# Finishing the last projections, and loading the gates, at other steps of a fused attention and FFN kernel

## The chip, the cores and the metric

The kernel runs on one core of one Trainium2 chip. The metric is the time of one execution on the device in microseconds (us), the median of several runs. TensorE (PE) multiplies matrices into PSUM; VectorE (DVE) and ScalarE (ACT) read PSUM and SBUF; GpSimd (POOL) works on SBUF; SyncE (SP) issues all DMA transfers of this kernel, one after the other, each after the waits that it carries.

## The reference

The input x has 1024 tokens of 512 channels. With xn = layernorm(x), the result is

```python
s = attention(xn)          # 32 query heads, 8 key/value heads, head size 128
g = silu(ffn(xn))          # dequantized gate, up and down matrices, 1792 wide
out = x + s * g
```

Attention normalizes queries and keys by RMS with weights, adds a linear bias in the distance of the positions (ALiBi) under a causal mask, and projects the heads' outputs by Wo. All is float32 in the reference. The kernel writes every float32 operand of a matmul as a sum of two 16-bit numbers, high and low, and multiplies three of the four products (`mm3`, lines 112 to 116).

## The kernel before

The work stands in three stages. The FFN comes first (until 217 us in the profile); its silu is written to the DRAM scratch `gd`. Then come twelve projections of 8 tiles each (128 tokens, 12 matmuls of 128x512): for each of four pairs of key heads one `kv` and two `q` projections, kv0, q0, q1, kv1 and so on to q7. Then comes attention in 256 steps; a step is one query tile of one head. The first eight steps are interleaved with the last two projections (q6 and q7), two tiles to a step.

**Weights of the next projection.** `prepare(k + 1, t)` (L672) is called ahead of tile t of projection k. It holds a small table by t: at t = 1 `norms` (ones times the squared weights, on PE, into a PSUM bank that `spare` (L486) gives, and `am`, the scale, on DVE), from t = 2 on `split_head`, one head a tile: ACT writes the high half `wh` (L561), DVE the low half `wl` (L562). `squares` for the projection after that runs on ACT at t = 6. The tiles of a projection use two PSUM tags of two banks each, "m" for even and "o" for odd tiles; `spare` takes a bank of "m" too.

**Finishing of a projection's tiles.** ACT copies a tile from PSUM to `f` (L580, three buffers of four tiles). `queue_half` (L767) then puts off, by counts of steps, `inverse` and `newton` (the reciprocal root of the norm), `normalize` (POOL, L636) and `halves` (DVE: the cast to the high half at L648, the subtraction to the low half at L649, into an `a16` buffer of five). For all but the last projection the pair is then transposed by DMA (L657) and stored to `qd` or `kd` (L662, L664). The last projection (q7, the queries of the last group of heads) is not stored: its pairs stay in SBUF until `last_queries` (L817) transposes them at the steps of `LAST_QUERIES`. When they are made is written out by hand in `LAST_ROOTS` and `LAST_PAIRS`, step numbers by half and by tile.

**Attention.** There are eight groups of heads of 32 steps each: group g has steps 32g to 32g + 31. A group takes four blocks of 256 queries (`qb`), in the order 2, 3, 0, 1 (group 7: 2, 3, 1, 0). Step n does: scores on PE (L114 to L116) into the PSUM tag "s"; one step later the minimum with the bias on DVE (L878, 256 instructions in all, by which a step can be found in the profile) and the exponential on ACT (L879); then the high half on ACT (L898) and the low half on DVE (L907) in a `p16` buffer of five; then a DMA transpose of the pair to `pT` (L915, or L910 for block 0, where POOL first clears a part of the buffer at L894); nine steps after the scores PE multiplies by the values (`av`). The output projection `op` follows, and DVE adds it to y.

**Gates.** For each block `gate_load(qb)` (L959) loads 0.5 MB of `gd` and 0.5 MB of x by two DMAs (L962, L963) at the step in `GATE_LOADS`, and `gate_partial` multiplies y by the gate and adds x, four POOL instructions (L969, L970) from the step in `GATE_SUMS`. Both lists follow the last group's order of blocks, 2, 3, 1, 0. A load uses one of the three `f` buffers. The order on each engine and in SP's queue is the program's own order; no scheduler changes it.

## Time and profile before

| what | value |
|---|---|
| time, three runs | 1067.37, 1065.36, 1066.66 us (median 1066.66) |
| profiled execution, own time | 1066.42 us |
| its span, first to last instruction | 1064.6 us |
| PE busy | 1002.7 us (94%) |
| DVE busy | 886.1 us (83%) |
| ACT busy | 802.7 us (75%) |
| POOL busy | 413.9 us (39%) |
| hardware DMA queue (SP) | 203.21 MB, 85.4% of 16 engines |

The page's first part gives the busy time of each engine, summed over all stages. PE is idle for 62 us of the span, and the question is where. The view by windows puts 17.3 us of that into the first 200 us (FFN), which the change does not touch; the rest lies in the projections, where attention fills up, and in the last 60 us.

The time outside the span is 1066.42 - 1064.6 = 1.8 us; it is taken as the same before and after.

### The profile page before, as it was taken

To read this page: it belongs to the slowest core of one execution; us is meant where nothing else is said; L and a number is where in the kernel's file an instruction comes from. 1 tells how busy PE (TensorE), PEld (TensorE's weight loads), DVE (VectorE), ACT (ScalarE), POOL (GpSimd) and SP (SyncE) were. 2 spreads that over 40 slices of the span, in tenths; PEclk is the share of its full clock that TensorE was granted. 3 is DMA by queue.
4 is the path that set the end of the run, shared out by engine and by line. 5 is a ranking of instruction groups with operands and counts; after the bars stand their busy time and mean duration, and the time that the engine had idled before them with its cause. 6 is when DMAs were issued, how large, how long until landed. Compare 5 with 4: busy or idle time off the path is not lost.

```text
span 1064.6 us, 18405 instructions
## 1 busy us (share of the span) xinstructions
PE 1002.7 (94%) x5913; PEld 584.6 (55%) x5913; DVE 886.1 (83%) x1745; ACT 802.7 (75%) x2160; POOL 413.9 (39%) x407
## 2 busy tenths in 40 slices
PE   7899899999989999898799999999999999999986
PEld 4344377844444444344566666566666666665563
DVE  7888996638778687788799899898998998979986
ACT  5777644778877787587778788797987888868862
POOL 2588653124545546361343215123141141250732
PEclk9999999999999999999999999999999999999998
DMA  6123259447988989989999999899999998999995
GB/s 202 49 100 119 70 170 302 166 139 162 219 228 188 242 203 235 279 179 207 226 193 214 195 200 222 167 227 197 189 207 193 197 223 182 221 224 194 231 189 129
DMA packets 455039, 204.39 MB, mean 192 GB/s; under 512 B 401506, under 2 KB 411038, under 8 KB 454942
## 3 DMA queue, kind: packets, MB, share of 16 engines
q1 hardware_dynamic: 454942, 203.21, 85.4%
q8 instruction: 46, 0.75, 0.3%
q14 instruction: 51, 0.42, 0.1%
HBM read 77.32 MB, written 27.27 MB: 98 GB/s over the span
## 4 chain that ended last, share of the span: by engine, by line
PE 48%; DVE 17%; ACT 13%; issue 10%; DMA 8%; SPq 2%; POOL 2%; DVEq 0%; ACTq 0%; POOLq 0%
PE gu_ps L267 6%; DMA pT<-p 4%; PE s L114 4%; DVE pf L878 3%; PE s L116 3%; PE s L115 3%; PE op L114 3%; PE op L115 3%; PE av L114 3%; PE op L116 3%; PE av L116 3%; PE av L115 3%; ACT p L898 2%; ACT pf L879 2%; PE ps_q L114 2%
## 5 line engine op out<-in xcount | busy, mean ns | idle before, releaser
L907 DVE SCALAR_TENSOR_TENSOR p<-pf,row,p 128x1024 f16<-128x1024 f32 (+7 forms) x256 | 227.8, 890 | 23.5 <-ACT p L898 20.3
L879 ACT ACTIVATE pf<-pf,row 128x1024 f32<-128x1024 f32 (+7 forms) x256 | 197.6, 772 | 57.2 <-DVE row L878 52.7
L878 DVE CUSTOM_DVE_ANT_0 pf<-s,trel,cs 128x1024 f32<-128x1024 f32 (+7 forms) x256 | 207.2, 809 | 13.7 <-PE s L116 13.4
L898 ACT ACTIVATE p<-pf,row 128x1024 f16<-128x1024 f32 (+7 forms) x256 | 196.5, 768 | 8.4 <-DMA pT<-p 3.5
L114 PE MATMUL av<-pT,vT 128*128 128x256 f16 (+1 forms) x640 | 167.8, 262 | 15.5 <-DMA pT<-p 15.5
L115 PE MATMUL av<-pT,vT 128*128 128x256 f16 (+1 forms) x640 | 167.8, 262 | 0.0
L116 PE MATMUL av<-pT,vT 128*128 128x256 f16 (+1 forms) x640 | 167.6, 262 | 0.0
L114 PE MATMUL s<-kT,qT 128*128 128x512 f16 (+3 forms) x384 | 125.0, 325 | 12.4 <-DVE row L878 12.1
L115 PE MATMUL s<-kT,qT 128*128 128x512 f16 (+3 forms) x384 | 125.0, 326 | 0.0
L116 PE MATMUL s<-kT,qT 128*128 128x512 f16 (+3 forms) x384 | 123.4, 326 | 0.0
L837 POOL TENSOR_SCALAR wor<-wor,rvs 128x512 f32<-128x512 f32 x32 | 54.5, 1702 | 162.8 <-DMA wor<-in_wo 141.5
L114 PE MATMUL ps_q<-wh_q,xth 128*128 128x512 f16 x256 | 97.6, 381 | 2.6 <-DVE am_q L526 2.5
L116 PE MATMUL ps_q<-wh_q,xtl 128*128 128x512 f16 x256 | 97.5, 381 | 0.0
L115 PE MATMUL ps_q<-wl_q,xth 128*128 128x512 f16 x256 | 97.5, 381 | 0.0
L114 PE MATMUL op<-woh,oh 128*128 128x512 f16 x248 | 94.5, 381 | 0.0
L115 PE MATMUL op<-wol,oh 128*128 128x512 f16 x248 | 94.3, 380 | 0.0
L116 PE MATMUL op<-woh,ol 128*128 128x512 f16 x248 | 94.2, 380 | 0.0
L114 PEld LDWEIGHTS <-vT 128*128 128x128 f16 x640 | 62.6, 98 | 56.6 <-DMA pT<-p 9.4
L115 PEld LDWEIGHTS <-vT 128*128 128x128 f16 x640 | 62.6, 98 | 41.3 <-issue 3.5
L941 ACT ACTIVATE oh<-av 128x256 f16<-128x256 f32 x128 | 47.7, 373 | 48.5 <-PE av L116 47.8
L636 POOL TENSOR_TENSOR f_q<-f_q,inv_q 128x512 f32<-128x512 f32 x64 | 77.4, 1237 | 1.1
L844 POOL TENSOR_TENSOR wol<-wor,woh 128x512 f16<-128x512 f32 x32 | 49.4, 1543 | 71.3 <-ACT woh L843 71.3
(194 smaller groups left out, 2255.6 us busy)
## 6 DMA issues: line engine op xcount, KB each, us to landing
qd<-tr_q SPq DMA_DIRECT2D x56, 256.0 KB, 3.4
qT<-qd SPq DMA_DIRECT2D x28, 512.0 KB, 4.5
wq<-in_wq SPq DMA_DIRECT2D x32, 256.0 KB, 3.9
wo_sq<-in_wo SPq DMA_DIRECT2D x8, 1024.0 KB, 9.1
wor<-in_wo SPq DMA_DIRECT2D x32, 256.0 KB, 3.7
gui<-in_gu_w SPq DMA_DIRECT2D x13, 512.0 KB, 3.5
wkv<-in_wkv SPq DMA_DIRECT2D x16, 256.0 KB, 3.8
vd<-v SPq DMA_DIRECT2D x8, 512.0 KB, 4.0
```

What stands on the lines that cost most here:

```text
L114: te.matmul(ps, lhsT=lh, rhs=rh, start=first, stop=False)
L115: te.matmul(ps, lhsT=lh, rhs=rl, start=False, stop=False)
L116: te.matmul(ps, lhsT=ll, rhs=rh, start=False, stop=last)
L267: te.matmul(banks[j][:, k, :], lhsT=w[:, j, ws], rhs=x[:, j, k * 512 : k * 512 + 512], start=x is xth, stop=x is xtl)
L636: ge.tensor_tensor(f, f, ib, ALU.mult)
L837: ge.tensor_scalar(wor[g, i], wor[g, i], rvs[:, g : g + 1], None, ALU.mult)
L844: ge.tensor_tensor(wol[g, i], raw, woh[g, i], ALU.subtract)
L878: ve.tensor_tensor_reduce(p, ps, trel[g][:, S - w :], cs[:, hh : hh + 1], 3e38, ALU.add, ALU.min, least[:, c])
L879: se.activation(p, p, AF.Exp, bias=least[:, c], scale=-1.0, accum_out=total[:, c])
L898: se.activation(p16[u, qt][:, :, 0, :], pf[u, qt], AF.Copy, scale=scale[:, qt : qt + 1])
L907: ve.scalar_tensor_tensor(lo, p, scale, hi, ALU.mult, ALU.subtract)
L941: se.activation(oh, av_ps[u], AF.Copy, scale=1.0 / P_SCALE)
```

## The change

It has five edits.

- `prepare`: every entry of the table but `squares` comes one tile later (`norms` at t = 2, `scale` at 3, `factors` at 7, `split_head` from 3, `split_values` from 5). The calls for projection 0, inside the FFN, are shifted by one so that they stay where they were.
- `spare`: the bank for `norms` is one of the scores' tag "s" for projections 1 to 10, and one of "o" for projection 11.
- `queue_half`: half 1 of q6 (the last but one projection, tiles 4 to 7) is finished at steps 28 (roots) and 36, 44, 52 and 60 (pairs), no more during q7. That moves its four DMA transposes and four stores as well.
- `LAST_ROOTS`, `LAST_PAIRS`: the roots of q7 move from steps 24 and 36 to 66 and 70, its pairs from 46, 78, 110, 142, 174, 221, 224, 229 to 76, 88, 100, 112, 124, 136, 148, 160. All eight are then held at once, so `halves` takes three of the buffers from the tag "tr", which nothing else uses by then.
- `GATE_LOADS`, `GATE_SUMS`, `gate_load`: loads for blocks 2, 3, 1, 0 at steps 194, 203, 211, 219 instead of 211, 219, 235, 251; sums at 221, 229, 244, 237 instead of 227, 235, 251, 259. Block 0's load has a buffer of its own.

```diff
-LAST_ROOTS = {1: 24, 0: 36}
-LAST_PAIRS = {4: 46, 5: 78, 6: 110, 7: 142, 2: 174, 3: 221, 0: 224, 1: 229}
+LAST_ROOTS = {1: 66, 0: 70}
+LAST_PAIRS = {4: 76, 5: 88, 6: 100, 7: 112, 2: 124, 3: 136, 0: 148, 1: 160}
+
+LATE_ROOTS = 28
+LATE_PAIRS = [36, 44, 52, 60]
...
-GATE_LOADS = [211, 219, 235, 251]
-GATE_SUMS = [227, 235, 251, 259]
+GATE_LOADS = [194, 203, 211, 219]
+GATE_SUMS = [221, 229, 244, 237]
...
     def spare(k, name):
-        return ps1("m", name) if k else pair(name)[:, 0, :]
+        if k == 0:
+            return pair(name)[:, 0, :]
+        return ps2(name)[:, 0, :] if k < len(projections) - 1 else ps1("o", name)
...
-                a16 = fq.tile([P, 2, n, HD], F16, tag="a16", name=f"q16_{self.i}_{t}", bufs=5)
+                tag = "tr" if self.k == len(projections) - 1 and t in (0, 1, 3) else "a16"
+                a16 = fq.tile([P, 2, n, HD], F16, tag=tag, name=f"q16_{self.i}_{t}", bufs=5)
...
-            elif t == 1:
+            elif t == 2:
                 p.norms()
-            elif t == 2:
+            elif t == 3:
                 p.scale()
-            elif t == 6:
+            elif t == 7:
                 p.factors()
-            if 2 <= t < 2 + p.n:
-                p.split_head(t - 2)
-            elif p.kind == "kv" and 4 <= t < 6:
-                p.split_values(t - 4)
+            if 3 <= t < 3 + p.n:
+                p.split_head(t - 3)
+            elif p.kind == "kv" and 5 <= t < 7:
+                p.split_values(t - 5)
...
         last = p is projections[-1]
+        late = p is projections[-2] and half == 1
 
         def due(steps, i, f):
-            if last and i is None:
+            if late:
+                c = TILES + (LATE_ROOTS if i is None else LATE_PAIRS[i] - 4)
+            elif last and i is None:
                 c = TILES + LAST_ROOTS[half]
...
-        gx = fq.tile([P, 2, NQT, DM], F32, tag="f", name=f"gx{qb}", bufs=3)
+        pool, tag, bufs = (fq, "f", 3) if qb else (late[0], "gx", 1)
+        gx = pool.tile([P, 2, NQT, DM], F32, tag=tag, name=f"gx{qb}", bufs=bufs)
```

More of the change, by code (lines that the diff above doesn't have):

```diff
@@ L707, in attention_gated_by_ffn_kernel @@
         if it == NI - 4:
-            prepare(0, 1)
+            prepare(0, 2)
         if it == NI - 3:
@@ L750, in attention_gated_by_ffn_kernel @@
                 elif NI - 6 <= it < NI - 1:
-                    prepare(0, 8 - NI + it)
+                    prepare(0, 9 - NI + it)
                 if it == NI - 2:
```

## The prediction

> **What bounds the kernel now.** Read first the page's busy times: PE works 1002.7 of 1064.6 us, so it is the bound nearly everywhere, and only PE's own idle time can be won. Next come PE's waits. Among the longest are:

> ```profile
> PE av L114 <- DMA pT<-p: 15.5, 14, 2.7
> PE s L114 <- DVE row L878: 12.1, 19, 1.8
> PE n_ps L518 <- DVE v L595: 5.6, 3, 2.7
> ...
> PE ps_q L114 <- DVE am_q L526: 2.5, 2, 1.2
> ```

> The last two are in the projections, the first two where attention fills up and at its end. The timeline of PE places them:

> ```profile
> 305.03 0.17 PE L518 MATMUL n_ps<-sb_q,ones_bf 128*128 128x4 bf16 x1 [1.46 <-DVE v L595]
> ...
> 309.05 0.38 PE L114 MATMUL ps_q<-wh_q,xth 128*128 128x512 f16 x1 [1.24 <-DVE am_q L526]
> ...
> 440.07 0.16 PE L518 MATMUL n_ps<-sb_q,ones_bf 128*128 128x4 bf16 x1 [2.71 <-DVE v L595]
> ...
> 440.50 0.63 PE L115 MATMUL ps_q<-wl_q,xth 128*128 128x512 f16 x1
> ```

> `norms` of the next projection stands between tiles 0 and 1 and wants a bank of "m" that tile 6 of the kv projection before still holds; then tile 2 waits for the bank of `norms`. The pair of waits comes again at 371.71 and 375.72.

> The steady groups of attention are read by windows, one a block of eight steps. Group 3 (steps 96 to 111):

> ```profile
> 685.54:702.04 16.50, 16.50 (x118) 10.47 (x117) 16.21 (x35) 15.07 (x33) 2.72 (x1) 1.00 1.05 207
> 702.04:725.08 23.04, 23.04 (x159) 14.58 (x157) 22.38 (x37) 19.76 (x35) 10.33 (x6) 1.00 1.07 218
> ```

> The columns are the window's length, then PE, weight loads, DVE, ACT and POOL busy, clock, DMA share, GB/s. PE is full, and DVE lacks only 0.29 and 0.66 us of it. In the other two blocks of the group DVE has 3.67 and 1.42 us left.

> **1. Projections.** PE's waits for banks after kv1, kv2 and kv3 are 1.46 + 1.24, the same again, and 2.71 us; with two of 0.26 us at other starts they are 8.6 us. After the last one the clock is 0.50 from 439.40 to 442.82, and the matmul takes 0.63 instead of 0.38 us. PE is busy 2.75 us there, so half of it, 1.4 us, is lost: 10.0 us in all. [...] This trace shows it halved after gaps of 2.71 us and of 2.66 us (below). [...] The wait itself goes: "s" is idle in projections 1 to 9, and for projection 11 the bank of "o" that is asked for at t = 2 was freed by tile 7 a tile earlier.

> What is late next is `wl`. Against the start of PE's next projection the last L562 ends 0.7 us early after each kv (300.08 for 300.82), and 2.75 to 4.2 us early elsewhere, 1.6 at q7. One tile is 2.59 us. The fourth head comes a tile later, but most of what stands ahead of it in DVE's queue was not waiting for PE: at t = 5 DVE has one L562 less to do before it, and the added step ahead of it is 0.42 + 0.41 + 0.69 us (L595, L648, L649) beside ACT's evacuation of a tile, about 1.1 us (L580, L582, L594). I put 0.7 us of new wait on each of q2, q4, q6 and q7's start, 3 us; ends 0 and 7. **Net -7 us**, ends -10 and -3.

> **2. Where attention fills up.** DVE and ACT, between steps 4 and 5:

> ```profile
> 478.82 1.25 DVE L648 CAST q<-f_q 128x512 f16<-128x512 f32 x1 [2.72 <-POOL f_q L636]
> 480.10 1.41 DVE L649 TENSOR_TENSOR q<-f_q,q 128x512 f16<-128x512 f32 x1
> 481.43 1.26 DVE L648 CAST q<-f_q 128x512 f16<-128x512 f32 x1
> ...
> 484.40 1.28 DVE L878 CUSTOM_DVE_ANT_0 pf<-s,trel,cs 128x1024 f32<-128x1024 f32 x1
> ...
> 485.72 1.15 ACT L879 ACTIVATE pf<-pf,row 128x1024 f32<-128x1024 f32 x1 [4.35 <-DVE row L878]
> ```

> DVE finishes q6's tiles 4, 5, 6 (5.6 us, after 2.7 us of waiting for POOL), and ACT idles 4.35 us for the minimum behind them. All of that leaves. PE pays for it later: its waits for L878 from 485.74 to 503.90 are 0.36, 0.80, 1.42, 1.82 and 0.28, together 4.7 us. The transposes' waits after that (505.49 to 522.68: 0.45, 2.57, 2.32, 0.38) stay: ACT stands 1.41 and 2.52 us before L843 for POOL's scaling of Wo, which waits for its load. q6's four transposes and four stores also leave SP's queue there. **-4 us**, ends -8 (part of the transposes' waits too) and 0 (ACT or the loads hold it all).

> **3. The pairs' new places.** A pair costs DVE 0.42 + 0.69 us in quiet, 1.26 + 1.41 while POOL works. Group 1 gets four and loses one. Two of them fall at steps 36 and 44, where DVE is nearly full, two into blocks with 3.8 and 1.4 us left; four transposes and four stores come too, each with an SP issue of about 1.3 and 0.6 us and landing 3 to 4 us later; nobody waits for them before group 6. **+0.8 us**, ends 0 and +3. Groups 2 to 5 get eight for four (+4.4 us of DVE); only 76, 100, 136 and 160 fall into full blocks, where 78, 110, 142 and 174 stood. **+0.5**, ends -2 and +3. Three leave groups 6 and 7: the block with step 221 takes 16.26 us and the one with 224 and 229 takes 17.37, where groups without them take 13.5 and 16.5. The gates' sums stay there, so of 3.6 us I count **-1.3**, ends -3 and 0.

> **4. Gates.** Two loads of 1 MB move from steps 235 and 251 into steps 194 and 203, ahead of transposes in SP's queue where the DMA share is 1.05 already. Next row: the load at 994.31 delayed the transpose behind it to 7.6 us from a usual 3 to 4. A transpose there has five steps (10 us or more) until PE needs it, so most is covered: **+1**, ends 0 and +4. Without the load at 994, the waits for pT at 1011.40, 1017.71 and 1024.37 (0.56, 1.26, 1.60) shrink: **-1.2**, ends -3 and 0.

> The last steps are on the path itself. SP's timeline, then the chain of waits:

> ```profile
> 1035.67 0.46 SPq L962 DMA_DIRECT2D gx<-gd  x1
> 1036.17 0.47 SPq L963 DMA_DIRECT2D gx<-in_x  x1
> 1037.14 1.23 SPq L910 DMA_TRANSPOSE pT<-p  x1
> ```

> ```profile
> 1036.66 0.48 POOL p L894 x2
> 1037.14 7.02 DMA pT<-p
> 1044.16 0.04 issue
> 1044.21 0.39 PE av L114
> ```

> Block 0's gates (1 MB) go out just ahead of unit 124's transpose, which lands after 7.0 us instead of 3.1 (the one at 1047.91). With 3.1 it would land at 1040.2, before PE is free at 1041.5. So the gap of 2.66 us goes, and with it the half clock that follows (1043.56 to 1046.98: PE busy 2.77, 1.4 lost): 4.0 us. For the wait after that, DVE must be faster too: from 1031 to 1046 its L907 and L984 take 1.41, 1.45, 1.41, 1.15 us where the same shapes take 0.73, 0.34, 0.48, 0.69, some 5.5 us over all, since POOL sums gates beside it and the clearings at L894 stand behind the sums. [...] But in 989.88 to 996.41, where four sums lie in a full block today, PE lost nothing (22.11 us long, 21.82 busy). [...] **-3.8 us**, ends -5 and -1.

> **Sum**, against the profiled execution's own 1066.4 us: -7.0 - 4.0 + 0.8 + 0.5 - 1.3 + 1.0 - 1.2 - 3.8 = -15.0, so **1051.4 us**. The median of the three runs is 1066.7, the same within 0.3.

> **Rivals.**
> - The tile's delay is paid in full. `wl` comes 2.59 us later after every kv: 1.9 us at three starts and 1 at q7 for my 3 us, and more where DVE is slowed by POOL, up to 7: **1055.4**. For it: DVE's L562 took 1.52 instead of 0.75 us at 294.54. Against: DVE idles 2.58 us for ACT at 304.55, so it isn't full.
> - The fill is held by ACT and the Wo loads, not by DVE: part 2 gives nothing, **1055.4** too. For it: ACT is busy 18.3 of 21.65 us from 494.32.
> - The end is not held by the gates' load: unit 124's transpose is slow because of the other traffic, part 4's last item gives 0.5 us: **1054.7**.
> - Slower: DVE becomes the bound of groups 1 to 5. Twelve pairs stand where five stood; at the contended 2.67 us each of the seven more puts 2.67 us on PE's path, 18.7 us in place of my 1.3: 1051.4 + 17.4 = **1068.8**. It decides from 2.3 us a pair on. For it: DVE lacks under 1 us in the first 40 us of each group. Against: group 3's last two blocks leave 5.1 us, and normalize runs two steps ahead, so POOL is mostly quiet at the cast.
> - The edits do not act: the bank of "o" for projection 11 waits like "m" did, and late pairs wait for POOL behind Wo's scaling. Then half is lost: **1059**.

> **Chances.** Forecast as summed 0.42; first two rivals 0.17 each; the end not helped 0.08; half lost 0.08; slower 0.08. The range reaches from part 1, 2 and 4 at their good ends together with the rest as taken (about 1044) to half lost with a little more (1061). A difference of 0.2% (2.1 us) is what can be told from no change; the cases give faster 0.88, same 0.04, slower 0.08.

> **What would show it.** PE starts tile 1 of q2 and q4 2.6 us after tile 0, and clock rows have no 0.50 near 440; a PE wait for `wl` at the start of q2, q4, q6, q7 is the first rival. ACT's wait of 4.35 us for L878 before step 5 is gone and PE's waits for L878 from 485 to 504 are under 1.5 us; else the second. Groups 1 to 5 stay within 1 us of 68.7 to 70.4 us; else the slower rival. The last block's av matmuls have no gap over 1 us. I am wrong in kind if PE's idle time only moves into the groups.

## The result, and the profile after

The changed kernel took **1076.72 us** (median of 4 runs, 1075.06 to 1078.2) where the kernel before took 1067.01 beside it: a ratio of **1.0083, 95% interval 1.0061 to 1.0106**. It is slower by 9 us; 15 us less were forecast. The profiled execution of the changed kernel spans 1073.8 us against 1064.6.

The two traces are cut at DVE's minimum of scores (L878 before, L888 after: the change adds lines) of steps 0, 32, 64, 192 and 224. "Projections" runs from PE's first projection matmul to step 0, "fill" is steps 0 to 31, the groups have 32 steps each, and "end" is group 7 with the tail.

| stage | before, us | after, us | difference | forecast |
|---|---|---|---|---|
| projections | 233.59 | 236.01 | +2.4 | -7 |
| fill | 95.87 | 91.77 | -4.1 | -4 |
| group 1 | 68.67 | 74.37 | +5.7 | +0.8 |
| groups 2 to 5 | 279.12 | 282.53 | +3.4 | +0.5 |
| group 6 | 72.06 | 78.93 | +6.9 | about 0 |
| end | 98.35 | 93.24 | -5.1 | -5 |

The differences sum to 9.2 us, so nothing lies elsewhere. What was to be won in the fill and at the end was won almost to the tenth; the other four stages, which were to gain 6 us together, lost 18.

PE's waits of the changed kernel (what it waited for: us in total, times, the longest):

```profile
PE av L117 <- DMA pT<-p: 20.3, 17, 3.0
PE s L117 <- DVE row L888: 10.4, 17, 1.7
PE ps_q L117 <- ACT wh_q L566: 7.2, 3, 3.7
PE ps_q L118 <- DVE wl_q L567: 3.8, 3, 1.3
```

The waits for banks in the projections are gone as forecast. In their place stand 11.0 us for heads, three times each: at the starts of q2, q4 and q6. And attention waits 4.8 us more for transposed probabilities than before (15.5). PE at the start of q4, from its timeline:

```profile
369.96 0.38 PE L117 MATMUL ps_q<-wh_q,xth 128*128 128x512 f16 x1 [3.73 <-ACT wh_q L566]
371.59 0.59 PE L118 MATMUL ps_q<-wl_q,xth 128*128 128x512 f16 x1 [1.25 <-DVE wl_q L567]
371.96 0.63 PE L119 MATMUL ps_q<-wh_q,xtl 128*128 128x512 f16 x1
...
374.45 0.38 PE L119 MATMUL ps_q<-wh_q,xtl 128*128 128x512 f16 x1
```

The kernel before lost 2.70 us in two waits here and kept its clock. Now it is 4.98 us, and a half clock from 370.96 to 374.37 (0.63 instead of 0.38 us a matmul).

The fill, DVE and ACT between steps 4 and 5:

```profile
478.09 1.26 DVE L917 SCALAR_TENSOR_TENSOR p<-pf,row,p 128x1024 f16<-128x1024 f32 x1
479.28 1.27 DVE L888 CUSTOM_DVE_ANT_0 pf<-s,trel,cs 128x1024 f32<-128x1024 f32 x1
...
480.08 1.10 ACT L889 ACTIVATE pf<-pf,row 128x896 f32<-128x896 f32 x1
```

No pair stands between them, and ACT's 4.35 us of waiting for the minimum is gone.

Windows (length, then PE, weight loads, DVE, ACT and POOL busy, clock, DMA share, GB/s; the DMA share adds up the times of all packets over the 16 engines, so it can pass 1). The third blocks of groups 1 and 6 in the kernel before:

```profile
585.34:601.62 16.28, 15.32 (x124) 11.20 (x123) 12.51 (x35) 12.46 (x37) 5.57 (x7) 1.00 1.12 213
...
932.49:950.04 17.55, 16.17 (x136) 12.14 (x135) 13.30 (x35) 12.20 (x36) 9.06 (x11) 1.00 1.10 221
```

The changed kernel: the third block of group 1, the first two blocks of group 3, and the second and third blocks of group 6:

```profile
583.89:604.79 20.90, 17.02 (x124) 11.69 (x122) 14.17 (x37) 12.52 (x37) 7.61 (x10) 0.92 1.14 213
...
691.09:708.35 17.26, 17.26 (x122) 10.86 (x121) 17.14 (x38) 15.18 (x33) 2.72 (x1) 1.00 0.99 196
708.35:730.43 22.08, 22.08 (x153) 14.02 (x152) 21.70 (x38) 20.77 (x38) 9.35 (x6) 1.00 1.06 226
...
918.70:940.65 21.95, 21.95 (x147) 13.47 (x146) 20.68 (x34) 19.51 (x35) 6.72 (x5) 1.00 1.17 260
940.65:965.79 25.14, 18.31 (x136) 12.66 (x135) 11.97 (x36) 12.37 (x36) 9.08 (x10) 0.93 1.11 212
```

Group 3 is bound as before, PE full and DVE within 0.4 us of it. The two third blocks are different, 4.6 and 7.6 us longer than before: in the last line every engine has 6.8 us or more without work and the mean clock is 0.93, while the DMA share is 1.11. Something off the engines is late there.

The end, from SP's timeline (L920 is the transpose of block 0, L910 before):

```profile
1047.11 1.23 SPq L925 DMA_TRANSPOSE pT<-p  x1
1049.52 1.24 SPq L920 DMA_TRANSPOSE pT<-p  x1
```

No load of gates stands ahead of block 0's first transpose any more, and it lands 3.06 us after its issue (7.02 before). After 1038 PE has no gap over 0.57 us, and the half clock from 1043.56 to 1046.98, put at 1.4 us lost (half of PE's 2.77 busy us in it, an estimate), is gone.

### The profile page after: what moved, and what is told of

It is laid out like the page before. It is cut to its first block, busy times and chain, and to the rows that moved or that the text cites. A ratio compares the mean times of both kernels' runs of the same rounds, so it can differ in the third digit from the quotient of the medians.

```text
span 1073.8 us, 18365 instructions
## 1 busy us (share of the span) xinstructions
PE 1006.3 (94%) x5913; PEld 585.3 (55%) x5913; DVE 880.4 (82%) x1745; ACT 802.0 (75%) x2160; POOL 406.0 (38%) x407
## 4 chain that ended last, share of the span: by engine, by line
PE 47%; DVE 19%; ACT 12%; issue 10%; DMA 9%; POOL 3%; SPq 1%; DVEq 0%; ACTq 0%; POOLq 0%
DMA pT<-p 7%; PE gu_ps L270 6%; DVE pf L888 4%; PE av L117 3%; PE ps_q L118 3%; PE ps_q L119 3%; PE ps_q L117 3%; PE av L119 3%; PE av L118 3%; PE s L117 3%; PE s L119 3%; PE s L118 3%; PE op L117 3%; PE op L118 3%; PE op L119 3%
## 5 line engine op out<-in xcount | busy, mean ns | idle before, releaser
L917 DVE SCALAR_TENSOR_TENSOR p<-pf,row,p 128x1024 f16<-128x1024 f32 (+7 forms) x256 | 223.6, 873 | 23.9 <-ACT p L908 20.6
L888 DVE CUSTOM_DVE_ANT_0 pf<-s,trel,cs 128x1024 f32<-128x1024 f32 (+7 forms) x256 | 206.8, 808 | 17.5 <-PE s L119 16.8
L117 PE MATMUL av<-pT,vT 128*128 128x256 f16 (+1 forms) x640 | 168.5, 263 | 20.3 <-DMA pT<-p 20.3
L956 DVE SCALAR_TENSOR_TENSOR ol<-av,oh 128x256 f16<-128x256 f32 x128 | 53.4, 417 | 28.1 <-ACT oh L951 27.9
```

Source lines behind the costliest of these rows:

```text
L117: te.matmul(ps, lhsT=lh, rhs=rh, start=first, stop=False)
L888: ve.tensor_tensor_reduce(p, ps, trel[g][:, S - w :], cs[:, hh : hh + 1], 3e38, ALU.add, ALU.min, least[:, c])
L917: ve.scalar_tensor_tensor(lo, p, scale, hi, ALU.mult, ALU.subtract)
L956: ve.scalar_tensor_tensor(ol, av_ps.pop(u), 1.0 / P_SCALE, oh, ALU.mult, ALU.subtract)
```

## The experiments

Each ran beside the kernel before on the same chip; ratios are to that kernel. The stages are those of one profiled execution each, the ratios those of all runs:

| kernel | ratio (interval) | projections | fill | group 1 | groups 2-5 | group 6 | end |
|---|---|---|---|---|---|---|---|
| prep_back | 1.0037 (1.0024-1.0049) | 233.18 | 90.09 | 74.43 | 283.64 | 78.84 | 92.02 |
| prep_only | 1.0058 (1.0044-1.0072) | 236.19 | 97.16 | 69.47 | 279.49 | 74.81 | 97.84 |
| spare_only | 0.9993 (0.9981-1.0004) | 233.80 | 95.28 | 68.85 | 278.84 | 72.73 | 98.29 |
| spare_f4 | 1.0005 (0.9993-1.0017) | 234.09 | 96.46 | 68.88 | 278.69 | 72.08 | 98.29 |
| root_late | 0.9977 (0.9969-0.9984) | 232.07 | 97.15 | 69.45 | 278.57 | 72.06 | 98.33 |
| q7_norms | 0.9974 (0.9965-0.9983) | 231.68 | 96.29 | 68.94 | 278.35 | 72.80 | 97.44 |
| gates_back | 1.0064 (1.0049-1.0079) | 235.86 | 93.28 | 73.25 | 283.03 | 70.22 | 99.80 |
| gates_light | 0.9994 (0.9981-1.0007) | 236.81 | 91.11 | 74.58 | 283.04 | 70.88 | 92.05 |
| late_back | 1.0082 (1.0061-1.0103) | 236.91 | 96.68 | 68.21 | 286.46 | 76.54 | 93.14 |
| late_half | 1.0067 (1.0044-1.0090) | 236.25 | 91.09 | 73.44 | 282.34 | 76.46 | 92.89 |
| late_third | 1.0050 (1.0031-1.0070) | 236.01 | 90.64 | 71.27 | 282.68 | 78.87 | 92.53 |
| pairs_light | 1.0061 (1.0047-1.0075) | 237.23 | 91.14 | 74.49 | 280.73 | 78.02 | 92.53 |
| all_light | 0.9949 (0.9932-0.9965) | 236.81 | 90.59 | 70.22 | 279.31 | 71.56 | 92.32 |
| light_prep | 0.9915 (0.9897-0.9934) | 234.46 | 89.75 | 70.22 | 279.23 | 71.05 | 93.10 |
| light_prep2 | 0.9886 (0.9868-0.9903) | 233.76 | 89.49 | 70.22 | 278.67 | 71.41 | 93.13 |
| light_root | 0.9847 (0.9831-0.9864) | 228.66 | 89.20 | 70.23 | 278.75 | 71.14 | 93.65 |
| light_keys | 0.9857 (0.9830-0.9883) | 228.67 | 91.43 | 70.22 | 278.55 | 70.99 | 94.05 |

A stage that an edit doesn't touch mostly repeats within about 1.5 us in the projections and the groups, 2 us in the fill, so differences below that are not read. Some traces are further off: up to step 0 light_root runs the same instructions as root_late and took 228.7 us for 232.1, group 6 of prep_only and of late_half lies 2.7 and 2.5 us from the kernel that each was made from, groups 2 to 5 of late_back 3.9. So a few us in one trace count only where other traces or the ratio agree.

### The tile of delay

prep_back is the changed kernel with this undone, prep_only the kernel before with this alone:

```diff
-            elif t == 2:
+            elif t == 1:
                 p.norms()
-            if 3 <= t < 3 + p.n:
-                p.split_head(t - 3)
+            if 2 <= t < 2 + p.n:
+                p.split_head(t - 2)
```

(with `scale`, `factors`, the values' split and the bank of `norms` moved likewise).

> The changed kernel with the projections' preparation (norms, heads, the bank of norms) as before. Theory A (the tile of delay costs more at q2, q4 and q6, where ACT's queue brings the fourth head late, than the banks' waits did): the first step's minimum of scores falls at about 450.6 us instead of 453.0, and the total is 2 to 3 us under the changed kernel's, about 1.006 of the time before. Rival (the delay is not to blame, or gains as I first said): the total stays at 1.008 or rises to 1.012.

> The kernel before with the change's preparation of the projections alone (norms at t = 2 in banks of s and o, heads from t = 3); gates, pairs and q6 as before. Theory A (the tile of delay costs more than the banks' waits did, by itself): from the first projection's start to the first step's minimum 236 to 237 us instead of 233.6, PE's waits at q2, q4 and q6 are for heads, total 1.002 to 1.005 of before. Rival (the loss in the projections comes only together with the other edits, or is chance): 233 to 234 us, 0.999 to 1.001.

Every profile with the delay has 235.9 to 237.2 us of projections (nine kernels), the four with the old steps and the old bank 233.2 to 234.5. Undone, 0.46% of the time comes back; alone, it costs 0.58%. So theory A holds, in both directions, and more is lost than was expected and than the projections show: of prep_only's 7.8 us in the profiled execution 2.6 are there, 1.3 in the fill and 2.7 in group 6, where nothing was edited. In that last piece PE waits 2.45 us for one transpose of the third block where it waited 1.38 before; why the transpose is later stays unexplained.

Why the heads come late is in ACT's and DVE's timelines of the changed kernel, just ahead of q4:

```profile
359.04 1.41 DVE L656 TENSOR_TENSOR q<-f_q,q 128x512 f16<-128x512 f32 x1
...
363.11 1.41 DVE L656 TENSOR_TENSOR q<-f_q,q 128x512 f16<-128x512 f32 x1
...
364.63 0.37 ACT L585 COPY f_kv<-ps_kv 128x256 f32<-128x256 f32 x1 [4.27 <-DVE q L656]
...
367.42 0.21 ACT L624 ACTIVATE inv_kv<-ms_kv 128x8 f32<-128x8 f32 x1 [1.63 <-DVE ms_kv L614]
367.53 0.70 ACT L566 ACTIVATE wh_q<-wq,am_q 128x512 f16<-128x512 f32 x1
...
369.16 0.74 ACT L566 ACTIVATE wh_q<-wq,am_q 128x512 f16<-128x512 f32 x1
```

The evacuation of kv's tile 4 waits 4.27 us for an `f` buffer, which DVE's halves of q3 free late (1.41 us each with POOL's normalizing beside them, 358.78 to 363.97, where the same line takes 0.69 at 366.62, with POOL quiet). Behind it in the kernel's order for ACT stand a square root and the third head; the fourth head, the last line, ends at 369.90, and PE, which has waited 3.73 us for it, begins at 369.96. With the old steps this head was ready, low half included, 0.7 us before PE wanted it.

### What holds the starts of q2, q4 and q6

Can the banks' waits be removed without the delay? spare_only, and then two of the links behind it, all on the kernel before:

```diff
-        return ps1("m", name) if k else pair(name)[:, 0, :]
+        if k == 0:
+            return pair(name)[:, 0, :]
+        return ps2(name)[:, 0, :] if k < len(projections) - 1 else ps1("m", name)
```

> The kernel before with one edit: the norms of projections 1 to 10 take a bank of s instead of m; no step moves. Theory A (the waits for banks can be removed without the delay): PE's waits n_ps and am_q at the three kv projections' ends go, no wait for a head takes their place, the half clock after kv3 goes too; the first step's minimum falls at about 442 us instead of 450.6, total 0.992 to 0.994 of before. Rival (what is behind the bank's wait is late anyway: the heads come through ACT's queue and PE waits for them in place of the bank): 448 to 451 us, total 0.997 to 1.000.

spare_f4 adds a buffer:

```diff
-                self.f[half] = fq.tile([P, HT, n, HD], F32, tag="f", name=f"f_{self.name}_{half}", bufs=3)
+                self.f[half] = fq.tile([P, HT, n, HD], F32, tag="f", name=f"f_{self.name}_{half}", bufs=4)
```

> The kernel before with the norms of projections 1 to 10 in a bank of s, and a fourth buffer for the projections' results f. Theory A2 (the bank's wait was only the last link: ACT's evacuation of a kv projection's tile 4 waits 2 to 4 us for an f buffer that DVE's halves free late, and everything behind it in ACT's queue, tiles 5 to 7 and the heads, comes late): ACT's wait for the f buffer goes, PE's waits at the starts of q2, q4 and q6 go, the first step's minimum falls at about 443 us instead of 450.6, and the total is 0.993 to 0.995 of before. Rival (DVE's own order, the sums of squares behind v and the halves, holds ACT and PE all the same): 448 to 451 us and 0.998 to 1.000.

root_late also moves a half's square root one step on:

```diff
-                se.activation(y, a, AF.Sqrt)
...
-            due(1, None, lambda: p.newton(half, True))
+            due(1, None, lambda: p.root(half))
+            due(2, None, lambda: p.newton(half, True))
```

> The kernel before with the norms of projections 1 to 10 in a bank of s, a fourth f buffer, and ACT's square root of a half's norms one step later (newton with it). Theory A3 (what is behind every one of these waits is ACT's queue, in which a square root waits up to 6 us for DVE, whose halves run at half speed beside POOL's normalizing; a step later DVE has done it): ACT's wait before the square root falls under 2 us, PE's waits at q2, q4 and q6 fall under 0.5 us each, the projections take 226 to 229 us instead of 233.6, total 0.993 to 0.996 of before. Rival (DVE is late by itself, and the wait moves to the next link): 232 to 234 us, 0.998 to 1.001.

spare_only and spare_f4 go to the rivals: the time is the same, and my two theories fall one after the other. The bank alone isn't the cause: PE comes to q6 1.9 us earlier (214.6 us after its first projection, 216.5 before), and there the wait of q7's `norms` for a bank of "m", which this edit leaves in place, grows from 2.71 to 4.25 us. Nor is the buffer. With four buffers ACT's wait is still there, at another instruction. ACT ahead of q4 in spare_f4:

```profile
365.31 0.21 ACT L621 ACTIVATE inv_kv<-ms_kv 128x8 f32<-128x8 f32 x1 [5.85 <-DVE ms_kv L611]
```

and in root_late:

```profile
362.46 0.21 ACT L625 ACTIVATE inv_kv<-ms_kv 128x8 f32<-128x8 f32 x1 [2.44 <-DVE ms_kv L611]
```

A square root of 0.21 us held ACT's queue 5.85 us for a sum that stands on DVE behind the slowed halves. One step later it is 2.44, and PE starts q6 211.8 us after the first projection instead of 216.5 (PE's timelines; 215.4 in spare_f4). That is the only edit of the three that shows in the time, 0.23%. Theory A3 holds for the waits at q2 and q4, but its sizes were missed: ACT's wait was to fall under 2 us, and the projections, 226 to 229 us expected, took 232.1, which is the rival's figure. Of the 4.7 us two are lost at once, since the tile at q6's start grows from 6.65 to 8.89 us, with 4.8 us of wait for `norms`.

q7_norms gives the last norms another bank and tile, light_keys (built on the best version below) sends the first group's keys, values and queries behind q7's weights instead of ahead:

```diff
-        return ps2(name)[:, 0, :] if k < len(projections) - 1 else ps1("m", name)
+        return ps2(name)[:, 0, :] if k < len(projections) - 1 else ps1("o", name)
...
-            elif t == 1:
+            elif t == (1 if k < len(projections) - 1 else 2):
                 p.norms()
```

> The kernel with the late square root, with the norms of the last projection alone at t = 2 in a bank of o (all others at t = 1 in s). Theory E (at q6's start PE waits 4.8 us only for the bank of m that kv3's tile 6 holds, and half a clock follows; with a bank that is free by then both go): the tile of q6's start takes 4 to 6 us instead of 8.9, the projections 228.5 to 230 us instead of 232.1, total 0.994 to 0.996 of before. Rival (what frees that bank, DVE behind ACT, is late for every bank): 8 us or more for that tile, or as much more at the next, total 0.997 to 0.999.

```diff
-        if k == len(projections) - 3:
-            load_keys(0)
...
+            if (k, t) == (len(projections) - 3, KT):
+                load_keys(0)
...
```

> The kernel with the lighter places and the later square root, with the first group's keys, values and queries loaded at tile 4 of the kv projection before q6 instead of ahead of its tile 0. Theory F (at q6's start PE waits for a bank behind ACT, which waits 3.9 us for the last quarter of q7's weights; that landed late because 1.5 MB of keys, values and queries were sent just ahead of it): ACT's wait for the weights goes, the tile at q6's start takes 4 to 5 us instead of 8.0, the projections 225 to 226 us instead of 228.7, total 0.981 to 0.983 of before. Rival (DVE, 3 us late with its sums of squares there, holds the bank just as long): 7.5 us or more for that tile, total 0.984 to 0.986.

Both rivals again. In q7_norms the first tile is short (3.72 us) and the next two take 5.88 and 7.61. PE in light_root, which still has the old order of loads, and ACT ahead of it:

```profile
429.44 0.63 ACT L512 ACTIVATE sq_q<-wq 128x512 bf16<-128x512 f32 x1 [3.86 <-DMA wq<-in_wq]
...
434.22 0.16 PE L523 MATMUL n_ps<-sb_q,ones_bf 128*128 128x4 bf16 x1 [4.10 <-DVE v L600]
```

and in light_keys:

```profile
434.84 0.58 PE L117 MATMUL s<-kT,qT 128*128 128x512 f16 x1 [4.53 <-POOL nwt_kv L634]
```

With the order turned round ACT's wait for the weights falls from 3.86 to 1.41 us, and PE waits as long, now for step 0's operands, which are the keys and queries that were sent later; the tile at q6's start takes 9.58 us for 8.04. (The trace names POOL as the releaser, but the load of the queries, issued at 427.48, landed after 7.06 us, at 434.54, just before PE began.) So one of the two transfers is late in either order, and what would relieve q6's start is open.

### The gates

gates_back undoes the fourth part on the changed kernel; gates_light keeps it and moves the loads alone:

```diff
-GATE_LOADS = [194, 203, 211, 219]
-GATE_SUMS = [221, 229, 244, 237]
+GATE_LOADS = [211, 219, 235, 251]
+GATE_SUMS = [227, 235, 251, 259]
```

(and the buffer of block 0 in `f` again), against

```diff
-GATE_LOADS = [194, 203, 211, 219]
+GATE_LOADS = [120, 152, 184, 216]
```

> The changed kernel with the gates' loads, sums and buffer as before. Theory B (two loads of 1 MB put into group 6, where the DMA queue is already full, cost 6 to 7 us there and win 5 at the end): group 6 goes from 78.9 us back to about 72, the end from 93.2 to about 98, and the total falls by 2 us, to about 1.006 of before. Rival (group 6 is late for another reason, the pairs' places or the throttle): group 6 stays near 79, the end gets 5 us longer, and the total is about 1.013 of before.

> The changed kernel with its gates' loads at steps 120, 152, 184 and 216, in the fourth blocks of groups 3 to 6, where the DMA share is about 0.7; sums and buffers as in the change. Theory B2 (the loads cost 7 to 9 us in group 6 only because the DMA queue is full there): group 6 takes 70 to 72 us instead of 78.9, groups 3 to 5 stay within 1 us, the end stays at 93, total about 1.000 to 1.002 of before. Rival (a megabyte more costs its time wherever it is put, or the sums on POOL are what costs): groups 3 to 6 together stay within 2 us of the 289.5 us they take now, total 1.006 to 1.009.

SP's timeline of the changed kernel in group 6 shows the two loads among the transposes:

```profile
906.70 0.58 SPq L973 DMA_DIRECT2D gx<-gd  x1
907.33 0.54 SPq L974 DMA_DIRECT2D gx<-in_x  x1
907.97 1.23 SPq L925 DMA_TRANSPOSE pT<-p  x1
909.25 1.68 SPq L809 DMA_DIRECT2D kT<-kd  x1
...
931.93 0.58 SPq L973 DMA_DIRECT2D gx<-gd  x1
932.56 1.40 SPq L974 DMA_DIRECT2D gx<-in_x  x1
934.07 3.15 SPq L925 DMA_TRANSPOSE pT<-p  x1
937.26 0.58 SPq L844 DMA_DIRECT2D wor<-in_wo  x1
```

Both follow theory B. With the old loads group 6 takes 70.2 us and the end 99.8; with three of the four loads in the fourth blocks of groups 3 to 5, whose DMA share was 0.72, 0.71 and 0.69 without them, group 6 takes 70.9 and the end keeps its 92. That one line of numbers is worth 0.9% (1.0083 to 0.9994), as much as the whole change had cost. Those three blocks are no longer for it (14.33, 15.39 and 13.49 us for 14.32, 15.40 and 13.49). Over all traces, group 6 takes 76.5 to 78.9 us in the six with loads at steps 194 and 203, and 70.2 to 71.6 in the seven built on the change without them. The sums on POOL stayed where the change put them, so what they cost is too small to be seen here: the rival falls. Group 6's third block in gates_light:

```profile
940.46:958.27 17.81, 16.16 (x136) 12.15 (x134) 12.62 (x35) 12.19 (x36) 8.00 (x9) 1.00 1.09 193
```

It is 7.3 us shorter than the same block of the changed kernel, with the same 136 matmuls in it.

### q6's late half

late_back takes it back:

```diff
-        late = p is projections[-2] and half == 1
+        late = False
```

> The changed kernel with the late half of q6 finished at once again, as before; the last queries' pairs stay at their new places. Theory C (the four late pairs cost group 1 its 5.7 us more, through their transposes and stores in SP's queue and DVE's halves that wait for POOL): group 1 goes back from 74.4 us to about 69, the stretch to step 32 gets 4 us longer again, and the total falls by 1 to 2 us, to about 1.007 of before. Rival (group 1 is late for the q7 pair and roots at steps 66 to 76 or for what came before): group 1 stays above 72 and the total rises by 2 to 4 us, to about 1.011.

Group 1 goes back to 68.2 us and the fill to 96.7: the move wins 4.9 us and costs 6.2, in the time (1.0082 to 1.0083) nothing that can be told. Theory C holds for its place; the total of about 1.007 that I expected lies inside its interval, and so does the changed kernel's 1.0083. Which of the four pairs?

```diff
-LATE_PAIRS = [36, 44, 52, 60]
+LATE_PAIRS = [36, 44, 82, 88]
```

(late_half, with the root at 70 moved to 90), and

```diff
-LATE_PAIRS = [36, 44, 52, 60]
+LATE_PAIRS = [50, 53, 56, 58]
```

> The changed kernel with the last two of q6's four late pairs moved from steps 52 and 60 to 82 and 88 (and the root of q7's lower half from 70 to 90, behind them); the first two stay at 36 and 44. Theory C1 (the third block of group 1 is late because the pair at 52 waits there for POOL, busy with Wo, and its transposes and stores meet the unit's own): steps 48 to 55 take 17 to 18 us instead of 20.9, group 1 69.5 to 71, group 2 at most 1.5 more. Rival C2 (the pairs at 36 and 44 in the blocks where DVE is full are what costs): group 1 stays at 73 or above.

> The changed kernel with all four late pairs of q6 at steps 50, 53, 56 and 58, behind POOL's work on Wo, in and next to the third block of group 1. Theory C3 (the place and not the number is what costs): group 1 takes 70 to 71.5 us instead of 74.4, total 1.005 of before. Rival C4 (four pairs with their transposes and stores are too many for one group wherever they stand): group 1 73 to 75 us, total 1.008.

The third block of group 1 in late_half, then PE's waits in it:

```profile
582.92:603.64 20.72, 15.36 (x124) 11.00 (x123) 12.57 (x35) 12.42 (x37) 5.64 (x8) 1.00 1.12 213
```

```profile
PE av L117 <- DMA pT<-p: 5.4, 3, 2.2
```

and in late_third:

```profile
581.35:599.56 18.21, 15.95 (x118) 11.50 (x117) 16.33 (x41) 11.77 (x35) 9.62 (x10) 0.91 1.10 210
```

My theory C1 fell, and C2 and C3 hold. In late_half no pair is in the block and it is as slow as with one, waiting for transposes; in late_third DVE does nearly 4 us more in it, and it is 2.5 us shorter. The pairs at 36 and 44 are the costly ones. The second block of group 1, in which the pair at 44 falls, is in the changed kernel, in late_back and before:

```profile
561.79:583.89 22.10, 21.62 (x148) 13.77 (x147) 22.07 (x38) 19.55 (x35) 8.00 (x5) 1.00 1.13 220
...
568.00:589.66 21.66, 21.66 (x149) 13.76 (x147) 21.36 (x36) 19.41 (x35) 8.53 (x5) 1.00 1.10 223
...
563.02:585.34 22.32, 21.58 (x148) 13.74 (x147) 21.99 (x37) 19.42 (x35) 8.96 (x6) 1.00 1.06 218
```

DVE has 0.03 us left in it (0.30 in late_back), so I took it that everything behind the pairs comes later, the probabilities and their transposes too, and that PE meets this a block later. The last line speaks against DVE's time as the whole reason: the kernel before has a pair in this block too, the one at 46, which is not transposed or stored, and its third block took 16.28 us with no wait for transposes. The pairs at 36 and 44 differ from it by their transposes and stores in SP's queue, and by being two. No run moved a pair without its transfers, so which of these makes the larger part is not shown.

### The last queries' pairs, and all places together

```diff
-LAST_PAIRS = {4: 76, 5: 88, 6: 100, 7: 112, 2: 124, 3: 136, 0: 148, 1: 160}
+LAST_PAIRS = {4: 82, 5: 88, 6: 114, 7: 120, 2: 146, 3: 152, 0: 178, 1: 184}
```

> The changed kernel with the last queries' eight pairs at steps 82, 88, 114, 120, 146, 152, 178 and 184, near the ends of the third blocks of groups 2 to 5, where DVE has 3 to 4 us left; all else as in the change. Theory D (a pair costs time only where DVE has none left): groups 2 to 5 together take 276 to 278 us instead of 282.5, total 1.002 to 1.004 of before. Rival (a pair costs its DVE time or its DMA wherever it stands): 281 to 284 us, total 1.007 to 1.010.

The truth lies between the two: groups 2 to 5 take 280.7 us, 1.8 less. Within a third block two pairs are still paid for:

```profile
800.24:817.87 17.63, 16.35 (x136) 12.17 (x135) 15.13 (x40) 12.20 (x36) 7.74 (x9) 1.00 1.09 206
```

DVE has 2.5 us left over the block, but PE waits 1.3 us in it for minima behind pairs (the same block of the kernel before, with none, took 16.41 us). Over a whole group little of that is left: groups 3 to 5 take 69.4 us with two pairs in these places, 69.2 to 70.0 before with one at their 14th step. What is over lies in group 2, 72.6 us for 70.4, where the roots stand at 66 and 70.

all_light moves everything at once, in numbers alone:

```diff
-LAST_ROOTS = {1: 66, 0: 70}
-LAST_PAIRS = {4: 76, 5: 88, 6: 100, 7: 112, 2: 124, 3: 136, 0: 148, 1: 160}
+LAST_ROOTS = {1: 66, 0: 90}
+LAST_PAIRS = {4: 114, 5: 120, 6: 146, 7: 152, 2: 178, 3: 184, 0: 210, 1: 216}
...
-LATE_PAIRS = [36, 44, 52, 60]
+LATE_PAIRS = [50, 56, 82, 88]
...
-GATE_LOADS = [194, 203, 211, 219]
+GATE_LOADS = [120, 184, 219, 152]
```

> The changed kernel with q6's late pairs at 50, 56, 82 and 88, the last queries' pairs at 114, 120, 146, 152, 178, 184, 210 and 216, and the gates' loads at 120, 184, 219 and 152: numbers only, no other edit. If the places alone were wrong: group 1 takes 69 to 71 us instead of 74.4, groups 2 to 5 276 to 279 instead of 282.5, group 6 71 to 73 instead of 78.9, the end stays at 93, and the total is 0.993 to 0.996 of before. Rival (the work moved costs the same wherever it stands in attention): total above 1.004.

It meets its expectation in every stage but groups 2 to 5 (0.3 us over), and at 1060.90 us the same edits now make the kernel faster than before.

### A version that beats both

light_prep is all_light with the projections' preparation as before; light_prep2 also has the root at 52 instead of 66; light_root adds the bank of s, the later square root and, in place of block 0's own buffer, a fourth `f` buffer.

> The changed kernel with the lighter places of pairs and loads (numbers as in the earlier run of them) and the projections' preparation as before. If the parts' costs add up: 0.9949 less the 0.0046 that the preparation alone gave back, 0.989 to 0.991 of before, about 1056 us. Rival (the parts share one wait, and one of them gives it back): 0.993 to 0.995.

> The same with the root of the last queries' upper half at step 52 instead of 66. Theory D (steps 64 to 71 have no DVE time left: they take 17.7 us with that root and 16.5 without, and the third block has): group 2 takes 70.2 us instead of 71.4, group 1 stays, total 0.001 under the run above. Rival (the root costs its time in the third block of group 1 too): groups 1 and 2 together stay within 0.5 us of the run above.

> The changed kernel with the lighter places of pairs, roots and loads, the preparation of the projections at its old steps with the norms of projections 1 to 10 in a bank of s, the later square root, and the gates' buffer made one of four f buffers. If the gains add up: 0.9886 less the 0.0023 that the late square root gave on the kernel before, 0.986 to 0.987, about 1053 us, with projections of 232 us and a fill of 89 to 90. Rival (what the projections win is lost where attention fills up, as it was on the kernel before, where the fill took 97.2 us for 95.9): 0.988 to 0.989.

light_prep gave 0.9915, a little less than the sum. light_prep2 is another 0.003 lower, but the intervals overlap, and its group 2 is only 0.5 us shorter and not 1.2, so the root explains a part of that at most. light_root reached **1050.41 us, 0.9847 (0.9831 to 0.9864)**, a little under the sum's 0.986 to 0.987, which the interval just touches. Its trace has 5.1 us less in the projections than light_prep2 and as short a fill, so the rival does not show; but root_late, with the same instructions up to step 0, had won 1.5 us there, so how much of the 5.1 is the edit and how much this one execution is not shown. PE's waits in it:

```profile
PE s L117 <- DVE row L891: 13.2, 19, 2.3
PE av L117 <- DMA pT<-p: 5.1, 4, 2.3
PE n_ps L523 <- DVE v L600: 4.1, 1, 4.1
```

The waits for transposes are a quarter of the changed kernel's 20.3 us.

## Why the prediction was wrong, step by step

**1. Projections, -7 forecast, +2.4 measured.** The waits that were to go did go. The failed step is "What is late next is `wl`" with 0.7 us of new wait at each start: it measured 11.0 us over q2, q4 and q6, and half clocks at q4 and q6 (from 370.96 and 439.22). I argued from DVE's queue alone. The heads come from ACT first (7.2 of the 11.0 us are for `wh`), and ACT's queue held, ahead of the fourth head, an evacuation and a square root that were waiting already in the trace of before:

```profile
361.40 0.37 ACT L580 COPY f_kv<-ps_kv 128x256 f32<-128x256 f32 x1 [2.28 <-DVE q L649]
...
365.15 0.21 ACT L619 ACTIVATE inv_kv<-ms_kv 128x8 f32<-128x8 f32 x1 [2.59 <-DVE ms_kv L609]
```

My rival "the tile's delay is paid in full" named the place, but laid it on `wl` alone, and at 7 us where it is 11 and these half clocks. And the 8.6 us of bank waits could not be won by the bank alone: spare_only has none of the old ones at q2 and q4 and is no faster.

**2. Fill, -4 forecast, -4.1 measured.** The mechanism is right: ACT's wait behind the pairs is gone, and late_back gives 4.9 us back. That the size fits so closely is in part luck. PE's waits for minima fell from 4.7 to 2.0 us and not to nothing (one of 1.75 us is left at 498.86), and the waits for transposes, which were to stay, fell from 5.9 to 4.5.

**3. The pairs.** The failed term is group 1's +0.8 (ends 0 and 3), which measured +5.7. I knew that 36 and 44 lie where DVE is nearly full, and priced them like the two others, with "nobody waits for them before group 6". Nobody waits for the pairs, but what is queued behind them and their transfers is waited for: late_half against late_back puts 5.2 us (73.44 to 68.21) on those two and their transfers. Groups 2 to 5 cost +3.4 for my +0.5. I had named the rival, DVE as the bound, and put its turning point at 2.3 us a pair. The pairs took a quiet 1.1 us each on DVE (0.42 and 0.69), and what decided was their place; whether through DVE or through SP's queue stays open. What the pairs' leaving gives group 6 was near: 72.06 to 70.22 us in gates_back, for -1.3.

**4. Gates.** The end is right: -5.1 for the -1.2 and -3.8 forecast, and the last transpose, the gap and the half clock went as said. The step that failed is the load's +1 (ends 0 and 4): it cost 8.0 us (78.93 to 70.88 in gates_light). I looked at the one transpose behind a load, and found five steps of room for it. But two megabytes delayed more than one transfer: behind the first megabyte the keys landed after 9.3 us and the next transpose after 8.6 (5.4 and 5.7 in gates_light), the second block ran at a DMA share of 1.17, the last of Wo's loads there went out 6 us later, and in the third block PE waited 6.8 us for four transposes (1.6 us for one in gates_light). That gates' sums on POOL beside a full DVE cost PE nothing, which I took from the row of 989.88 to 996.41, held: PE has no idle time in steps 232 to 239 (22.62 us, DVE busy 22.17) with 12.1 us of POOL beside it, 6.2 of them gates' sums.

**The sum.** Of -15.0, parts 2 and 4's end (-9) came. Part 1 missed by 9.4 us, part 3 by 8, the loads by 7. The three misses are alike: a cost was looked for at the instruction that moves, and not in the queue that it joins. By my own sign ("wrong in kind if PE's idle time only moves into the groups") that is in the main what happened: PE's idle time fell from 10.6 to 6.6 us in the fill, and rose from 1.9 to 4.8 in group 1 and from 2.4 to 7.8 in group 6. The lower end of my range was also added wrongly: parts 1, 2 and 4 at their good ends give 1040.4, not about 1044; nothing hangs on it.

## What to carry to other kernels

Before moving work under "idle" time, take from the trace, for every queue that it joins (the engine's own order, SP's, and the transfers in flight), how much is left in that very block. Here two loads of 1 MB cost 5 to 9 us where the DMA share was 1.05 and 1.06 without them and nothing that could be seen where it was 0.69 to 0.72, and two pairs of 1.1 us, with their transfers, cost 5.2 us in blocks where DVE lacked 0.5 us or less of the whole. The same edits were worth +9 or -6 us by their step numbers alone. And where a wait goes and the time stays, follow its releaser back link by link: here the bank and the buffer gave nothing, the square root behind them 0.23%, and the transfer behind that is still open.
